# Dense attention rows by quarters of an image row, and a gate computed ahead of layer-norm statistics

## The chip, the cores and the metric

The kernel runs on one core of a Trainium2 chip. The time is that of the device, in microseconds: the median of several executions of the whole program. One further execution was taken with the hardware profiler; durations of single instructions come from it.

A core has a matrix engine (TensorE, "PE" in the profile, its weight loads "PEld"), a vector engine (DVE), a scalar engine (ACT), GpSimd (POOL), and SyncE (SP), which here only starts transfers. Transfers are started from SP's queue and from ACT's (SPq and ACTq) and carried out by 16 DMA engines. Each engine works through its own instructions in order and waits for the others by semaphores. A matmul multiplies a stationary operand, loaded first (LDWEIGHTS), with a moving one and writes to PSUM.

## The reference

The program is a chain of four blocks over `x[4, 64, 64, 128]`, all in float32. Two stages of it matter here. The first is the deformable attention of the first block: for each of 4 groups of 32 channels, a 3x3 neighbourhood with dilation `dil = 2 * i + 1` is shifted by learned offsets, keys and values are sampled there by bilinear interpolation, and a softmax over the 9 taps weighs the values.

```python
off = conv1x1(pconv(q_img, pconv_off_w[i]), w_off[i], b_off[i])
dil = 2 * i + 1
k_list.append(deform_sample(kv[0, :, i], off, mask, dil, dil * PAD))
v_list.append(deform_sample(kv[1, :, i], off, mask, dil, dil * PAD))
...
attn = jax.nn.softmax(jnp.einsum('bgnc,bgckn->bgnk', qf, ks_), axis=-1)
out = jnp.einsum('bgnk,bgckn->bgnc', attn, vs_)
...
return out @ w_proj + b_proj
```

The second is a triangle multiplication on the pair representation: `a` and `b` are gated projections of the normalized input `z`, `u` is their product summed over an index, and the output is the normalized `u` times `w_out`, times the sigmoid of `z @ w_gate`.

## The kernel before, in words

**Projection of the deformable part** (`deformable_project`). It computes queries, keys, values and offsets for the 4 images and stores them to DRAM: `qd`, `kd`, `vd`, `od`. `vd` holds the values with the image column first and a padded image row second, each row of 64 columns as two halves of 32; padding rows are zeroed at the start by ACT's queue (20 transfers), and the values are stored by ACT's queue, too (line 569, 8 stores per image).

**The local part** (`deformable_near`, about 660 to 1935 us in the profile). A test on the device takes this branch where all offsets are small. The unit of work is T, 128 queries: two image rows of 64. There are 32 per image, 128 in all, and four of them make a group c. The 128 partitions hold the queries as (column half h, row r, column in the half).

1. `products`, `product`, `copy_products`: queries times the keys around them. `product` (line 749) runs 64 small matmuls (32 x 32 stationary, 108 to 216 columns moving) per T, in two halves, into four PSUM tiles `S`; ACT copies them to `band` (line 759).
2. `hats`, `hat_products` (POOL): interpolation weights `H` from the offsets `of`.
3. `attention`, `spread` (DVE, one exponential on ACT): logits, softmax, and the 3 x W weights `A` of each query.
4. `write` (SP, line 821, 16 transfers per c): scatters `A` to the DRAM tiles `dd`, each query's weights at its own place on a row of zeros, so that they become a dense row over image columns. The rows cover 64 columns and some padding. `dd` is zeroed once at the start from a zeroed part of `dense` (line 665, 32 transfers).
5. `read_dense` (line 835): brings the dense rows back to SBUF for two T at once, as `dense` (tiles `D`): 8 transfers, 4 from SP's queue and 4 from ACT's, each of 64 partitions and 204 to 240 KB.
6. `transpose` (line 864): 24 transposes per T (three tap rows ty, two column halves, four groups), through PSUM tiles `pt`, copied by ACT to `dt` (line 866, six copies of 128x512).
7. `value_block` (line 845): loads a block of 4 image rows of values as `vb` (512 KB, one transfer, contiguous runs of 4 KB; 20 blocks per image, 9 buffers).
8. `weigh` (line 876): 24 matmuls of 128 rows (4 image rows of 32 columns: the columns of one half) x 32 channels x 128 queries per T, accumulated in `out` in PSUM. A float32 matmul shows as two records of the profile.
9. `values_done`, `projection`, `store`: once per c the output is copied, multiplied with `w_proj` (line 898), added to the input with POOL, and stored by SP (line 907). The result tile `pr` uses the transposes' PSUM buffers `pt`.

The order on each engine is written out by hand. Step T of the loop starts the loads and the DVE, POOL and ACT work that is due (`step`), then runs on PE, twice, once per half: transposes of T - LAG, product of T, projection if one is ready, weigh of T - LAG. `LAG = 13` is the distance between products and values. Before the first values the loop runs products alone, and after the last product, values alone (the drain).

**Triangle** (`stage_triangle`, about 2270 to 2670 us). Two passes `pr` over two images each: `zT` is the transposed normalized input, `u` is computed on PE, DVE takes its statistics (lines 1228 and 1229, 64 of each), PE transposes the normalized `u` (line 1241), and then for 16 groups PE computes `pg = zT * w_gate` and `po = uT * w_out` (lines 1253 and 1254), ACT the sigmoid `s` of `pg` (line 1259), DVE `s * po` (line 1260) and POOL adds it to `xs` (line 1261).

## Time and profile before

| what | value |
|---|---|
| median of 3 executions | 7821.81 us (7803.61 to 7821.86) |
| profiled execution | 7794.26 us, span 7792.5 us |
| mean granted TensorE clock | 0.907 of full |
| PE, DVE, ACT, POOL busy | 86%, 61%, 37%, 22% of the span |
| first transposes of the local part | 776 us |
| last product of the local part | 1835 us |
| end of the local part's values | about 1935 us |
| triangle's last stretch (second pass) | 2637 to 2668 us |

The page gives for the whole span the busy time of each engine, the granted clock and the DMA share in 40 slices of 195 us (slices 4 to 10 are the local part), the groups of instructions by line, and the transfers by queue. Since stages differ in what limits them, a stage is read through its own window: the busy time of each engine in 100 us, the waits by line inside it, and the sequence of work on PE. A row of the timeline begins with the start in us and the length in us. In a row by line, the last part is the time the engine stood idle just ahead of the group, with what released it; "issue" means that nothing in the profile shows what it waited for.

### The profile page before, as it was taken

To read this page: it belongs to the slowest core of one execution; us is meant where nothing else is said; L and a number is where in the kernel's file an instruction comes from. 1 tells how busy PE (TensorE), PEld (TensorE's weight loads), DVE (VectorE), ACT (ScalarE), POOL (GpSimd) and SP (SyncE) were. 2 spreads that over 40 slices of the span, in tenths; PEclk is the share of its full clock that TensorE was granted. 3 is DMA by queue.
4 is the path that set the end of the run, shared out by engine and by line. 5 is a ranking of instruction groups with operands and counts; after the bars stand their busy time and mean duration, and the time that the engine had idled before them with its cause. 6 is when DMAs were issued, how large, how long until landed. Compare 5 with 4: busy or idle time off the path is not lost. (4 is left out here: it accounts for less than half of the span.)

```text
span 7792.5 us, 166207 instructions
## 1 busy us (share of the span) xinstructions
PE 6724.8 (86%) x67663; PEld 3662.9 (47%) x67663; DVE 4726.2 (61%) x11050; ACT 2881.2 (37%) x6529; POOL 1720.3 (22%) x1638
## 2 busy tenths in 40 slices
PE   7985888897668878979999999798798897997989
PEld 3343666675445555335555555444325224243244
DVE  2113555553447743858866666575685885867877
ACT  3421444444324432731126565475204013031056
POOL 0004343331001110015542222144112012121135
PEclk9997999999678989989999999799798997998989
DMA  4346777876140013030100000001111111111101
GB/s 111 93 107 197 186 198 189 205 199 171 55 144 1 2 37 62 8 116 22 26 18 9 10 10 9 9 1 29 35 26 40 33 25 48 26 37 38 25 22 30
DMA packets 655282, 508.22 MB, mean 65 GB/s; under 512 B 302662, under 2 KB 594441, under 8 KB 650665
## 3 DMA queue, kind: packets, MB, share of 16 engines
q1 hardware_dynamic: 454158, 350.46, 17.4%
q10 hardware_dynamic: 200346, 146.97, 7.4%
q8 instruction: 540, 8.85, 0.5%
q14 instruction: 238, 1.94, 0.1%
HBM read 340.52 MB, written 156.58 MB: 64 GB/s over the span
## 5 line engine op out<-in xcount | busy, mean ns | idle before, releaser
L2457 DVE TENSOR_TENSOR t<-S,q 128x1536 f32<-128x1536 f32 (+3 forms) x608 | 1157.0, 1948 | 121.1 <-PE S L2445 115.8
L2445 PE MATMUL S<-R,L 32*128 32x512 f32 x4096 | 734.4, 651 | 91.0 <-DMA R<-wd 79.8
L2473 PE MATMUL acc<-t,sum 128*32 128x512 f32 x4096 | 639.7, 608 | 0.0
L866 ACT COPY dt<-pt 128x512 f32<-128x512 f32 x768 | 404.0, 594 | 440.9 <-PE pt L864 337.5
L768 DVE COPY_PREDICATED band<-bit,band 128x288 f32<-128x288 int32 (+11 forms) x384 | 246.1, 754 | 434.2 <-ACT band L759 434.2
L2159 PE MATMUL pe<-ew,yT 128*128 128x512 f32 x1024 | 480.6, 604 | 25.1 <-DVE xs L2165 22.2
L1758 PE MATMUL acc<-w,attT 128*64 128x264 f32 x4096 | 486.0, 391 | 12.2 <-DVE w L1754 12.2
L2445 PEld LDWEIGHTS S<-R,L 32*128 32x128 f32 x4096 | 200.8, 187 | 612.0 <-issue 281.5
L749 PE MATMUL S<-kpad,qm 32*32 32x108 f32 (+3 forms) x16384 | 380.3, 323 | 119.2 <-issue 51.9
L2479 ACT COPY agg<-acc 128x512 f32<-128x512 f32 x32 | 18.7, 585 | 1194.3 <-DMA L<-pd 682.2
L864 PE MATMUL pt<-ident,D 128*128 128x128 f32 x3072 | 441.7, 297 | 5.1 <-issue 2.9
L864 PEld LDWEIGHTS pt<-ident,D 128*128 128x128 f32 x3072 | 389.4, 199 | 60.8 <-issue 46.7
L1751 POOL TENSOR_TENSOR w<-xtl,ei 128x528 f32<-128x528 f32 x256 | 331.7, 1317 | 313.7 <-ACT ei L1750 202.9
L2165 DVE SCALAR_TENSOR_TENSOR xs<-pe,gate,xs 128x128 f32<-128x128 f32 x1024 | 332.6, 345 | 97.0 <-PE pe L2159 80.3
L1754 DVE TENSOR_TENSOR w<-xtl,pe 128x1056 f32<-128x1056 f32 x256 | 320.3, 1251 | 101.6 <-ACT ei L1750 89.5
L1758 PEld LDWEIGHTS acc<-w,attT 128*64 128x64 f32 x4096 | 284.1, 137 | 198.5 <-DVE w L1755 37.9
L2168 ACT ACTIVATE sc<-pe,gate 128x128 f32<-128x128 f32 x1024 | 290.4, 374 | 200.2 <-PE pe L2159 193.1
L749 PEld LDWEIGHTS S<-kpad,qm 32*32 32x32 f32 x16384 | 234.3, 106 | 198.6 <-issue 97.9
L512 PE MATMUL dw<-pad,diag 32*32 32x512 f32 x6912 | 307.4, 616 | 10.5 <-ACT dwo L520 5.8
L2488 POOL TENSOR_TENSOR o<-o,bf 128x512 f32<-128x512 f32 x32 | 40.6, 1269 | 1230.4 <-ACT o L2487 1230.4
L2473 PEld LDWEIGHTS acc<-t,sum 128*32 128x32 f32 x4096 | 92.9, 108 | 457.6 <-issue 435.2
L2159 PEld LDWEIGHTS pe<-ew,yT 128*128 128x128 f32 x1024 | 186.1, 194 | 231.5 <-issue 151.2
(520 smaller groups left out, 12848.3 us busy)
## 6 DMA issues: line engine op xcount, KB each, us to landing
vb<-vd SPq DMA_DIRECT2D x80, 512.0 KB
w<-in_e_weight_dram ACTq DMA_DIRECT2D x16, 1024.0 KB
w<-in_e_weight_dram SPq DMA_DIRECT2D x16, 1024.0 KB
wd<-s SPq DMA_DIRECT2D x32, 512.0 KB
D<-dd ACTq DMA_DIRECT2D x64, 240.0 KB
D<-dd SPq DMA_DIRECT2D x64, 240.0 KB
D<-dd ACTq DMA_DIRECT2D x64, 228.0 KB
D<-dd SPq DMA_DIRECT2D x64, 228.0 KB
```

The lines of the kernel that those rows point to most:

```text
L512: nc.tensor.matmul(acc[g][32 * c : 32 * c + 32], diag[r, j, tap, :], pads[j][r, y0 : y0 + 8, tx : tx + 64], start=(tap == 0), stop=(tap == 8),
L749: ins = nc.tensor.matmul(acc[g][32 * j : 32 * j + 32].rearrange("p (a s) c -> p a s c", a=3), qm[rows, j, m, :], keys, start=(m == 0), sto ...
L864: ins = nc.tensor.transpose(pt[:, g, :], D[g][:, T % 2, q0 : q0 + 382 : 3], k.ident)
L866: nc.scalar.copy(dt, pt)
L1751: nc.gpsimd.tensor_tensor(w2[:, 2:4], xt[:, 2:4, 0:2], window(ei, 0, [[0, 2], [0, 2], [1, 132]]), op=ALU.mult)
L1754: nc.vector.tensor_tensor(w1, xt[:, :, 1:3], window(pe, 0, [[0, 4], [0, 2], [1, 132]]), op=ALU.mult)
L1758: nc.tensor.matmul(acc[b // 2][64 * (b % 2) : 64 * (b % 2) + 64], attT[:, b // 2, hp, 64 * (b % 2) : 64 * (b % 2) + 64], src[:, b].rearran ...
L2159: nc.tensor.matmul(pe[h].rearrange("p e c -> p (e c)"), yT[:, 128 * t : 128 * t + 128], ew[:, 4 * h : 4 * h + 4, :].rearrange("p e c -> p ...
L2165: nc.vector.scalar_tensor_tensor(xt, pe[0][:, e, :], gate[:, t, e : e + 1], xt, op0=ALU.mult, op1=ALU.add)
L2445: nc.tensor.matmul(S[:, j, :], Ls[n % 2][r, ag, :], Rs[n % 2][r, ag].rearrange("p x y -> p (x y)"), start=True, stop=True)
L2457: nc.vector.tensor_tensor(t[:, j0:j1].rearrange("p u (x y) -> p u x y", x=8), S[:, j0:j1].rearrange("p u (x y) -> p u x y", x=8), qf[:, q0 ...
L2473: nc.tensor.matmul(acc[0][32 * h : 32 * h + 32, :], sum4, t[:, j, :], start=(u < 4), stop=(u >= 60))
```

## The change

Two independent parts.

*Local part.* The dense rows now cover 32 columns for 16 query columns (a quarter of an image row) in place of 64 for 32, so that the rows are 12 * (15 + W) numbers apart plus 12 in place of 12 * (64 + W). `read_dense` runs for each T: 4 transfers, one per group, on all 128 partitions, two from SP's queue and two from ACT's; the source is 8 blocks of 16 rows, with an offset of a whole row more from block to block. `dense` is four tiles, one per T. A T has 12 transposes and three copies. `weigh` runs 48 matmuls of 32 queries (two runs of 16), one per quarter, tap row and group, and leaves out those whose image rows lie outside. `vd` has the columns with 8 of padding on both sides, so that the 32 columns around each quarter are one stretch; `value_block` loads the four quarters by four transfers of 256 KB (runs of 2 KB), 17 blocks per image, 7 buffers. On PE a step is now: transposes, both halves of the product, projection, weigh. `LAG` is 14. The zeroing of `dd` and of `vd` and the stores to `vd` change with the layouts.

*Triangle.* The 64 `pg` matmuls of a pass and the sigmoids move from the last loop to the place ahead of `u`'s statistics; the sigmoid is written over `zT`, which gets a second buffer, and the tile `s` is gone.

```diff
--- before.py
+++ after.py
@@ -382,7 +382,7 @@
-        vd = [dr.tile([32, 84, 2, 128], F32, tag=f"vd{b}", name=f"vd{b}") for b in range(4)]
+        vd = [dr.tile([80, 84, 128], F32, tag=f"vd{b}", name=f"vd{b}") for b in range(4)]
         od = [dr.tile([128, 32, 81], F32, tag=f"od{b}", name=f"od{b}") for b in range(4)]
@@ -453,11 +453,13 @@
                 nc.vector.tensor_copy(wcen[0:32, :], pe[0:32])
         with tc.tile_pool(name="dp_z", bufs=1) as zp:
-            zero = zp.tile([32, 1024], F32, tag="zero", name="zero")
+            zero = zp.tile([64, 1536], F32, tag="zero", name="zero")
             nc.vector.memset(zero, 0.0)
             for b in range(4):
-                for r0, n in ((0, 4), (4, 4), (72, 4), (76, 4), (80, 4)):
-                    nc.scalar.dma_start(vd[b][:, r0 : r0 + n].rearrange("w r h c -> w (r h c)"), zero[:, 0 : 256 * n])
+                for c0 in (0, 72):
+                    nc.scalar.dma_start(bass.AP(vd[b].tensor, vd[b].offset + c0 * 10752, [[1536, 56], [1, 1536]]), zero[0:56])
+                for r0, n in ((0, 8), (72, 12)):
+                    nc.scalar.dma_start(vd[b][8:72, r0 : r0 + n].rearrange("w r c -> w (r c)"), zero[:, 0 : 128 * n])
@@ -565,10 +567,10 @@
                         vt[:, :, i, :].rearrange("p j (g c) -> p j g c", g=4), pt.rearrange("p g (j c) -> p j g c", j=4)
                     )
                 d = vd[b]
-                for yh in range(4):
+                for r in range(2):
                     nc.scalar.dma_start(
-                        bass.AP(d.tensor, d.offset + 256 * (32 * half + 8 + yh // 2) + 128 * (yh % 2), [[21504, 32], [512, 16], [1, 128]]),
-                        vt[32 * yh : 32 * yh + 32].rearrange("p j i c -> p (j i) c"),
+                        bass.AP(d.tensor, d.offset + 8 * 10752 + 128 * (32 * half + 8 + r), [[10752, 64], [256, 16], [1, 128]]),
+                        vt[64 * r : 64 * r + 64].rearrange("p j i c -> p (j i) c"),
                     )
             off = sm.tile([128, 32, 81], F32, tag="off", name="off")
     nc, tc = k.nc, k.tc
     DIL = (1, 3, 5, 7)
     W = [2 * d + 3 for d in DIL]
     WB = [5, 9, 15, 21]
     CW = [w + 7 for w in W]
-    PP = [12 * (64 + w) for w in W]
+    PP = [12 * (15 + w) for w in W]
@@ -653,16 +656,17 @@
-        dd = [[dr.tile([128, 4, PP[g]], F32, tag=f"dd{i}{g}", name=f"dd{i}{g}") for g in range(4)] for i in range(2)]
-
-        dense = [[wp.tile([128, 2, 768], F32, tag=f"D{i}{g}", name=f"D{i}{g}") for g in range(4)] for i in range(2)]
-        for t in dense[0] + dense[1]:
+        dd = [[dr.tile([128, 4 * PP[g] + 12], F32, tag=f"dd{i}{g}", name=f"dd{i}{g}") for g in range(4)] for i in range(2)]
+
+        dense = [wp.tile([128, 4, 384], F32, tag=f"D{i}", name=f"D{i}") for i in range(4)]
+        for t in dense:
             nc.gpsimd.memset(t, 0.0)
         for i in range(2):
             for g in range(4):
-                zero = dense[i][g].rearrange("p t n -> p (t n)")
-                for t in range(4):
-                    (nc.sync, nc.scalar)[g % 2].dma_start(dd[i][g][:, t, :], zero[:, 0 : PP[g]])
+                zero = dense[g].rearrange("p t n -> p (t n)")
+                eng = (nc.sync, nc.scalar)[g % 2]
+                eng.dma_start(dd[i][g][:, 0 : 4 * PP[g]], zero[:, 0 : 4 * PP[g]])
+                eng.dma_start(dd[i][g][:, 4 * PP[g] : 4 * PP[g] + 12], zero[:, 0:12])
@@ -817,66 +821,74 @@
             for g in (1, 2, 3, 0):
                 d, P = dd[c % 2][g], PP[g]
                 for j in range(4):
-                    h, r = divmod(j, 2)
+                    r = j % 2
                     nc.sync.dma_start(
                         bass.AP(
-                            d.tensor, d.offset + 32 * j * 4 * P + 3 * r + 12 * 32 * h, [[4 * P + 12, 32], [P, 4], [1, 12 * W[g]]]
+                            d.tensor, d.offset + 32 * j * (4 * P + 12) + 3 * r, [[4 * P + 12, 32], [P, 4], [1, 12 * W[g]]]
                         ),
                         A[g][32 * j : 32 * j + 32, :, 0 : W[g]].rearrange("p t c s a -> p t (c s a)"),
                     )
-        def read_dense(T2):
-
-            c, t2 = divmod(T2, 2)
+        def read_dense(T):
+            c, t = divmod(T, 4)
             for g, d in enumerate(DIL):
-                n = 12 * (33 + d)
-                for h in range(2):
-                    rows, c0 = slice(64 * h, 64 * h + 64), (768 - n) * h
-                    (nc.sync, nc.scalar)[h].dma_start(
-                        dense[T2 % 2][g][rows, :, c0 : c0 + n],
-                        dd[c % 2][g][rows, 2 * t2 : 2 * t2 + 2, 12 * (d + 1) + c0 : 12 * (d + 1) + c0 + n],
-                    )
+                m, P = dd[c % 2][g], PP[g]
+                (nc.sync, nc.scalar)[g % 2].dma_start(
+                    dense[t][:, g, 12 * (7 - d) : 12 * (7 - d) + P],
+                    bass.AP(m.tensor, m.offset + t * P, [[16 * (4 * P + 12), 8], [4 * P, 16], [1, P]]),
+                )
         def value_block(n):
-            b, kb = divmod(n, 20)
-            t = sm.tile([128, 4, 2, 128], F32, tag="vb", name="vb", bufs=9)
+            b, kb = divmod(n, 17)
+            kb += 1
+            t = sm.tile([128, 4, 4, 128], F32, tag="vb", name="vb", bufs=7)
             d = vd[b]
-            nc.sync.dma_start(
-                t.rearrange("p i h c -> p (i h c)"), bass.AP(d.tensor, d.offset + 4 * kb * 256, [[21504, 32], [256, 4], [1, 1024]])
-            )
+            for q in range(4):
+                nc.sync.dma_start(
+                    t[:, q].rearrange("p s c -> p (s c)"),
+                    bass.AP(d.tensor, d.offset + 16 * q * 10752 + 4 * kb * 128, [[10752, 32], [128, 4], [1, 512]]),
+                )
             vblocks[b, kb] = t
         def values(T):
             b, i = divmod(T, 32)
-            for n in range(len(vblocks), min(80, 20 * b + (2 * i + 14) // 4 + 1 + max(2, i - 27))):
+            for n in range(len(vblocks), min(68, 17 * b + min(17, (2 * i + 14) // 4) + max(2, i - 28))):
                 value_block(n)
             if T % 4 == 0:
                 outs[0] = ps.tile([128, 4, 128], F32, tag="out", name="out")
-        def transpose(T, half):
-            D = dense[T // 2 % 2]
+        def transpose(T):
+            D = dense[T % 4]
             lefts[T] = []
-            for q in range(3 * half, 3 * half + 3):
+            for ty in range(3):
                 pt = ps.tile([128, 4, 128], F32, tag="pt", name="pt", bufs=3)
-                q0 = 384 * (q % 2) + q // 2
                 for g in range(4):
-                    ins = nc.tensor.transpose(pt[:, g, :], D[g][:, T % 2, q0 : q0 + 382 : 3], k.ident)
+                    ins = nc.tensor.transpose(pt[:, g, :], D[:, g, ty : ty + 382 : 3], k.ident)
                 dt = sm.tile([128, 4, 128], F32, tag="dt", name="dt", bufs=4)
                 nc.scalar.copy(dt, pt)
                 lefts[T].append(dt)
             return ins
-        def weigh(T, half):
+        def weigh(T):
             b, i = divmod(T, 32)
-            for q in range(3 * half, 3 * half + 3):
-                ty, h = divmod(q, 2)
-                for g, d in enumerate(DIL):
+            taps = {}
+            for g, d in enumerate(DIL):
+                for ty in (1, 0, 2):
                     kb, si = divmod(2 * i + (ty - 1) * d - 1 + 8, 4)
-                    ins = nc.tensor.matmul(
-                        outs[0][32 * g : 32 * g + 32, T % 4, :], vblocks[b, kb][:, si, h, 32 * g : 32 * g + 32], lefts[T][q % 3][:, g, :],
-                        start=(q == 0), stop=(q == 5),
-                    )
+                    if 1 <= kb <= 17:
+                        taps.setdefault(g, []).append((ty, kb, si))
+            quarter = lambda ap, q: ap.rearrange("p (h r q x) -> p h q r x", h=2, r=2, q=2)[:, q // 2, q % 2]
+            for q in range(4):
+                for n in range(3):
+                    for g in range(4):
+                        if n < len(taps[g]):
+                            ty, kb, si = taps[g][n]
+                            ins = nc.tensor.matmul(
+                                quarter(outs[0][32 * g : 32 * g + 32, T % 4, :], q), vblocks[b, kb][:, q, si, 32 * g : 32 * g + 32],
+                                quarter(lefts[T][ty][:, g, :], q), start=(n == 0), stop=(n == len(taps[g]) - 1),
+                            )
+            del lefts[T]
             return ins
         def values_done(T):
@@ -912,7 +924,7 @@
             if 0 <= n < 128 and n % every == 0:
                 do(n // every)
-        LAG = 13
+        LAG = 14
@@ -928,19 +940,19 @@
                 step(T, 4, attention, 4)
                 step(T, 7, spread, 4)
                 step(T, 9, write, 4)
-                step(T, LAG - 2, read_dense, 2)
+                step(T, LAG - 2, read_dense)
                 step(T, LAG, values)
             V, P = 0 <= T - LAG, T < 128
             late = list(stores)
-            for half in range(2):
-                if V:
-                    block(transpose, T - LAG, half)
-                if P:
-                    block(product, T, half)
-                if project:
-                    block(projection, *project.pop())
-                if V:
-                    block(weigh, T - LAG, half)
+            if V:
+                block(transpose, T - LAG)
+            if P:
+                block(product, T, 0)
+                block(product, T, 1)
+            if project:
+                block(projection, *project.pop())
+            if V:
+                block(weigh, T - LAG)
             with behind():
                 if late:
                     store()
@@ -1168,7 +1180,7 @@
             nc.scalar.dma_start(vec[:, i : i + 1], v.unsqueeze(1))
         for pr in range(2):
-            zT = big.tile([128, 2, 4096], F32, tag="zT", name="zT")
+            zT = big.tile([128, 2, 4096], F32, tag="zT", name="zT", bufs=2)
             for i in range(2):
                 b = 2 * pr + i
                 mv, r = k.ln_stats(sm, b, k.eps6)
@@ -1222,6 +1234,16 @@
                         else:
                             nc.vector.tensor_copy(dst, pu[rows])
+
+            gate = lambda im, g: zT[:, im, 512 * g : 512 * g + 512].rearrange("p (t c) -> p t c", t=4)
+            for im in range(2):
+                for g in range(8):
+                    pg = ps.tile([128, 4, 128], F32, tag="psA", name="pg")
+                    for j in range(4):
+                        t = 4 * g + j
+                        nc.tensor.matmul(pg[:, j, :], zT[:, im, 128 * t : 128 * t + 128], wg, start=True, stop=True)
+                    nc.scalar.activation(gate(im, g), pg, AF.Sigmoid)
+
@@ -1246,17 +1268,14 @@
             for im in range(2):
                 b = 2 * pr + im
                 for g in range(8):
-                    pg = ps.tile([128, 4, 128], F32, tag="psA", name="pg")
                     po = ps.tile([128, 4, 128], F32, tag="psU", name="po")
                     for j in range(4):
                         t = 4 * g + j
-                        nc.tensor.matmul(pg[:, j, :], zT[:, im, 128 * t : 128 * t + 128], wg, start=True, stop=True)
                         nc.tensor.matmul(
                             po[:, j, :], uT[:, im, 2 * t : 2 * t + 2, :].rearrange("p i j -> p (i j)"), wo,
                             start=True, stop=True,
                         )
-                    s = sm.tile([128, 4, 128], F32, tag="s", name="s")
-                    nc.scalar.activation(s, pg, AF.Sigmoid)
+                    s = gate(im, g)
                     nc.vector.tensor_tensor(s, s, po, op=ALU.mult)
                     nc.gpsimd.tensor_tensor(k.xs[b][:, 4 * g : 4 * g + 4, :], k.xs[b][:, 4 * g : 4 * g + 4, :], s, op=ALU.add)
```

## The prediction

> **What bounds the kernel now.** I read the page's time slices first, then the windows by stage, the PE timeline inside one window, the groups by line, the waits, the queues, and last the triangle's timeline. Changes of 0.3% or less (23 us) count as no change: about what a measurement of this kernel can tell.
>
> The deformable part's loop runs from 776 us (first transposes) to 1835 us (last product): 1059 us for 115 steps T, 9.2 us each. Windows of it (columns: length, busy time of PE, PEld, DVE, ACT, POOL, granted clock, DMA share, GB/s):
> ```profile
> 1000.00:1100.00 100.00, 89.74 (x2305) 69.56 (x2300) 55.70 (x146) 49.70 (x122) 45.93 (x58) 1.00 0.82 208
> 1300.00:1400.00 100.00, 89.06 (x2224) 69.97 (x2224) 52.51 (x142) 48.22 (x119) 38.93 (x58) 0.93 0.79 204
> 1835.00:1935.00 100.00, 77.91 (x1040) 56.20 (x1040) 18.64 (x54) 46.73 (x92) 14.36 (x10) 0.96 0.60 146
> ```
> PE is busy for 86 to 90% with DMA close behind at 0.8; DVE and ACT have half their time free. One undisturbed half step on PE:
> ```profile
> 1319.02 1.63 PE L864 MATMUL pt<-ident,D 128*128 128x128 f32 x12
> 1320.58 1.33 PE L749 MATMUL S<-kpad,qm 32*32 32x108 f32 x64
> 1321.84 0.86 PE L876 MATMUL out<-dt,vb 128*32 128x128 f32 x24
> 1322.63 1.63 PE L864 MATMUL pt<-ident,D 128*128 128x128 f32 x12
> ```
> Start to start: transposes 1.56, product 1.26, weigh 0.79; a half is 3.61, a step 7.2, with a quarter of the projection (1.08 per four steps) 7.5. The other 1.7 us of 9.2 are a granted clock under 1 (about 0.5 per step, from the clock rows) and stalls of PE, among them a refill of its instructions (the rows ending in "issue" below) and what waits for late transfers:
> ```profile
> L866 ACT COPY dt<-pt 128x512 f32<-128x512 f32 x588 | 309.1, 594 | 342.2 <-PE pt L864 265.2 <-DMA vb<-vd 55.0 <-DMA D<-dd 20.2
> L749 PE MATMUL S<-kpad,qm 32*32 32x108 f32 (+3 forms) x12547 | 280.9, 311 | 39.6 <-issue 39.5
> L876 PE MATMUL out<-dt,vb 128*32 128x128 f32 x4704 | 183.9, 287 | 18.3 <-issue 18.1
> L898 PE MATMUL pr<-wpj,oT 128*128 128x128 f32 x192 | 35.5, 340 | 42.7 <-ACT dt L866 40.7 <-issue 2.0
> ```
> (900 to 1800 us; last columns: busy, mean ns, idle before and releaser.) ACT waits 75 us for `vb` and `D`, and the projection, which shares the transposes' PSUM buffers, pays 41 us of it.
>
> **The loop, part by part.** *PE.* Per step 12 transposes go instead of 24: one 1.56 stays. The product's 128 records stay, in one piece: 2.3 (2x1.26 less one change of kind of matmul, 0.2 to 0.27). Weigh has 96 matmul records of N=32 for 48 of N=128. No row shows N=32. Upper bound: what a record takes now, 0.79 less a change, 0.2, over 24 records = 25.7 ns, 2.5 us per step; lower: four records on four row groups start about 7 ns apart in the records, 0.7 us. The nearest row is the product, also small matmuls on column groups, 64 in 0.99 us = 15.7 ns: 1.5+0.2 = 1.7 us. With the projection's 0.27: 1.56+2.3+1.7+0.27 = 5.8 us (5.0 to 6.6), plus the clock's 0.4: 6.2.
>
> The Trainium skill, "TensorE: Matmul & The Clock Gate", section "Back-to-back issue gap", puts a floor of about 25 ns under each small matmul. By it weigh costs 2.4 us and a step 0.7 more; the records at 7 and 15.7 ns on separate groups disagree, so I do not follow it.
>
> *Instructions.* A step has 48+256+96 = 400 matmul and weight-load records now and 24+256+192 = 472 then. The profile's instruction queue and its kind in 900 to 1800 us:
> ```profile
> q1 hardware_dynamic: 144403, 129.92, 56.3%
> q10 hardware_dynamic: 28198, 44.54, 20.5%
> q8 instruction: 155, 2.54, 1.3%
> ```
> (packets, MB, share.) 155 fetches serve 900/9.2 = 98 steps, 1.6 each, one per about 250 records. Stops of PE recur at that count; two fetches are never closer than 3.3 us and 5.8 us apart on average. After: 1.6x472/400 = 1.87 per step. At 3.3 us that is 6.2, at 3.9 it is 7.3, at the loop's mean 5.8 it is 10.9; but the mean includes time PE was slow for other reasons, so it is no latency. I take 3.9.
>
> *DMA.* Reads of `D` fall from 909 to 639 KB per step; `vb` grows from 80 transfers of 512 KB to 272 of 256 KB (41 to 71 MB in the stage). Packets get smaller: `D` runs of 960 to 1536 B for 1632 to 1920 B, `vb` 2 KB for 4 KB. Summed by the mean time of packets of near sizes (1920 B 132 ns, 1296 B 70, 816 B 50, 4 KB 215), the load per step goes from 7.2 us of each engine to 6.2 (5.4 to 6.7). But the new source pattern of `D` has 8 as its outermost size where the old one had 64 rows. The trace has one place with such a pattern, pair attention's loads `L` and `R` from 8 rows (5700 to 5900 us):
> ```profile
> q10 hardware_dynamic: 9216, 1.58, 4.1%
> L<-pd ACTq DMA_DIRECT2D x64, 8.0 KB
> R<-wd ACTq DMA_DIRECT2D x32, 32.0 KB
> ```
> 9216 packets are 64x64 and 32x128 of data and 1024 = 64x8+32x16 of four bytes that close each engine's share: `L` ran on 8 engines, not 16. If `D` does so, those 8 carry its 3.4 to 4.6 us per step, 1.4 to 2.0 of `vb` and some 2 to 2.2 of the rest: 6.8 to 8.8, the other 8 about 3.8. Middle 7.8.
>
> The skill's "DMA: Bandwidth & Descriptors", section "Why a DMA increments its semaphore by 16 and not by 1", says the number of engines is the largest up to 16 that divides the outermost sizes of both sides. By it `D` is on 8, which would make the upper half of that bound sure; it speaks against the change.
>
> *Others.* ACT loses three of six 594 ns copies: -1.8 of 5.6 us per step. Its two `D` issues (0.59 each, 127 us for 196) stay per step on average, but every step instead of four every second. DVE is untouched: 55% of 9.2 is 5.1 per step. SP gets 192 more `vb` issues at 0.54 (104 us over 128 steps, 0.8 each) on 4.5: 5.3. It now waits in other places:
> ```profile
> SPq L821 <- DMA D<-dd: 117.0, 132, 3.1
> SPq L907 <- POOL xg L901: 97.4, 24, 7.7
> SPq L835 <- PE pt L864: 94.4, 82, 4.4
> ```
> The writes' wait for old reads of `dd` (117 us in 900) remains, as does the wait for PE. `vb` has 7 buffers where 5 are live: its issue waits for weigh two steps back, and behind it on SP queue the `D` reads and the stores. Price: none while `D` is read two steps ahead; up to one transfer's lateness per block (2 us per two steps, 1 per step) if that cover is gone.
>
> The bounds stand close together: PE 6.2, fetch 7.3, eight engines 7.8, SP 5.3. A loop with several near-equal resources now runs 9.2 where its largest single one, PE with its clock, is 8.0; taking a smaller slip on a bound of 7.8 I get 8.0 (7.2 to 9.8). 114 steps x 8.0 = 912 for 1059: **-147**.
>
> **Around the loop.** *Drain* (1835 to 1935): 13 steps in 100 us, 7.7 each. Without product, transposes 1.56, a copy's wait 0.6, weigh 1.7, projection 0.3: 4.2 by PE, 6.0 by the 8 engines (`D` and `vb`). 14 x 5.1 = 72: **-28** (-10 to -40).
>
> *Prologue.*
> ```profile
> 665.66 32.88 SPq L665 DMA_DIRECT2D dd<-D  x16
> 698.95 4.12 PE L749 MATMUL S<-kpad,qm 32*32 32x108 f32 x128 [20.13 <-ACT band L759]
> ```
> Zeroing `dd` holds both issue queues for 32 us (14.7 MB at 398 GB/s); ACT's first copy waits behind it and PE with it. It becomes 5.1 MB, 13 us: -18. One more step of lag, +6: **-12** (-18 to 0).
>
> *Start.* `vd` zeroing grows from 2.6 to 5.4 MB beside first loads that fill the engines at 243 GB/s; stores of `vd` halve in number, on ACT, 0.7 each. **+4** (-2 to +10).
>
> *Triangle.*
> ```profile
> 2598.11 3.96 PE L1253 MATMUL pg<-wg,zT 128*128 128x128 f32 x32
> 2617.49 2.27 PE L1241 MATMUL ptu<-ident,u 128*128 128x128 f32 x8 [15.42 <-DVE u L1238]
> 2637.20 6.51 PE L1254 MATMUL po<-wo,uT 128*128 128x128 f32 x40 [1.32 <-ACT uT L1242]
> L1261 POOL TENSOR_TENSOR xs<-xs,s 128x512 f32<-128x512 f32 x16 | 20.2, 1271 | 167.7 <-DVE s L1260 167.6
> ```
> While DVE takes u's statistics PE waits 15 us; the 16 `pg` groups (0.9 each, 14.4 us) fit there. PE starts the first few already, limited by two PSUM buffers. The end, 2637 to 2667, then has `po` alone: about 15 us of PE in the first pair, POOL's 20.3 in the second for 29. Gain 13+8 less a little of the 4 us done early: **-20** (-28 to -8). If the sigmoids delay ACT, the square root behind them is next.
>
> **Sum.** -147-28-12+4-20 = -203. The profiled execution has 7794.3 us (span 7792.5), 27.6 under the median of the runs shown: 7591 against it, 7619 as a median.
>
> **Rivals.**
> 1. *The eight engines saturate* (step 9.2, by the upper end 8.8 plus 0.4 clock): loop -10, total about -65, 7757. For it: `L`'s 8 shares. Against: half the `D` bytes per step are gone.
> 2. *PE and DVE set the step*, weigh near 7 ns, 7.2 us: loop -238, drain -36, total about -300, 7520. Against it: fetches at 7.3.
> 3. *Slower: instruction refill bounds PE.* 1.87 fetches per step at 5.45 us, as in crowded stretches, make 10.2: loop +104, others -38, 7888. It decides from 9.7 us a step (114x9.7 = 1106, +47, which eats the rest). For: refills share engines with `D`. Against: they are as long as the engines are crowded, and bytes fall.
> 4. *No net change*: step about 9.7.
>
> **Chances.** Forecast 0.45, rival 1 0.17, rival 2 0.17, rival 3 0.15, rival 4 0.06: faster 0.79, same 0.06, slower 0.15. The range runs from rival 2 with the triangle's and drain's best ends (7500) to a step of 9.7 to 9.8 (7850); the forecast's own, steps of 7.6 to 8.6, is 7570 to 7690.
>
> **What would show it.** Weigh's 96 records in 1.5 to 1.9 us; transposes of successive steps 7.6 to 8.6 us apart; per-engine packet counts split over 8 engines for `D`; PE stops at refills; zeroing of `dd` in 13 us; `pg` inside the statistics. Wrong if weigh takes 2.5 us, or ACT's copies wait for `D` or `vb` more than 0.75 us a step.

## The result

The change makes the kernel faster: 7718.5 us median of 4 executions (7702.8 to 7738.1) for 7818.3 us (7803.6 to 7821.9), a ratio of 0.9877 with a 95% interval of 0.985 to 0.9904, or 99.8 us. The forecast was 7619 us: the direction was right and the time lies inside the range, but the gain is half of the one forecast.

The two profiled executions differ by only 56 us (spans 7792.5 and 7736.3 us), because the one before was 24 us under its median and the one after is 20 us above its own. Most of that difference sits in stages which the change doesn't touch, the last row here. From the first matmul of a stage to the first of the next:

| stage | before | after | difference |
|---|---|---|---|
| projection of the deformable part | 660.5 | 674.1 | +13.6 |
| local part | 1287.3 | 1191.3 | -96.0 |
| expert choice (unchanged) | 309.4 | 305.1 | -4.3 |
| triangle | 395.4 | 378.3 | -17.1 |
| recurrent (unchanged) | 216.9 | 233.1 | +16.2 |
| all that follows (unchanged) | 4908.4 | 4939.9 | +31.5 |

The table's first five rows sum to -87.6 us; the last row is the scatter of the two executions (the same stages, with the code of before, take 4931.8 us in tri_only). Inside the local part the prologue (first product to first transposes) went from 100.9 to 81.4 us, the loop (to the last product) from 1060.9 to 996.2, the drain (to the last weigh) from 88.7 to 77.2. A step of the loop takes 996.2/114 = 8.74 us for 9.23.

Windows of the loop after, with the columns as before:

```profile
1000.00:1100.00 100.00, 72.76 (x2660) 58.58 (x2662) 46.87 (x147) 31.48 (x86) 45.93 (x58) 0.91 0.74 212
1300.00:1400.00 100.00, 70.76 (x2645) 55.92 (x2648) 50.96 (x159) 30.05 (x85) 41.64 (x55) 0.90 0.76 211
```

PE is busy for 71 to 73 us of 100 in place of 89, no other engine is over 51, DMA is at 0.75. Nothing is full, and yet a step takes 8.7 us. The timeline of PE shows what it does in the rest:

```profile
1216.79 2.83 PE L867 MATMUL pt<-ident,D 128*128 128x128 f32 x12
1219.55 2.70 PE L753 MATMUL S<-kpad,qm 32*32 32x108 f32 x128
1222.18 1.42 PE L887 MATMUL out<-dt,vb 128*32 128x32 f32 x91
1225.22 0.26 PE L887 MATMUL out<-dt,vb 128*32 128x32 f32 x5 [1.62 <-issue]
1225.41 1.63 PE L867 MATMUL pt<-ident,D 128*128 128x128 f32 x12
1226.97 2.10 PE L753 MATMUL S<-kpad,qm 32*32 32x108 f32 x110
1230.53 0.60 PE L753 MATMUL S<-kpad,qm 32*32 32x216 f32 x18 [1.46 <-issue]
1231.07 1.16 PE L910 MATMUL pr<-wpj,oT 128*128 128x128 f32 x8
1232.15 1.03 PE L887 MATMUL out<-dt,vb 128*32 128x32 f32 x96
```

PE stops in the middle of a row of equal matmuls, with nothing that the profile shows to wait for ("issue"), and it does so at every 255 or so records of matmuls and weight loads: here at about 1223 and 1229 us. An uninterrupted weigh (the last row) takes 1.0 us for 96 records. From the groups by line, 900 to 1700 us:

```profile
L753 PE MATMUL S<-kpad,qm 32*32 32x180 f32 (+3 forms) x11648 | 272.4, 338 | 76.9 <-issue 61.7 <-POOL qm L722 9.2 <-ACT band L763 4.6
L867 PE MATMUL pt<-ident,D 128*128 128x128 f32 x1083 | 183.1, 327 | 17.5 <-ACT o L912 10.8 <-issue 4.8 <-DMA D<-dd 1.8
L869 ACT COPY dt<-pt 128x512 f32<-128x512 f32 x273 | 148.1, 612 | 94.8 <-PE pt L867 94.1
L887 PE MATMUL out<-dt,vb 128*32 128x32 f32 x8477 | 123.1, 207 | 111.0 <-issue 110.9
L763 ACT COPY band<-S 128x108 f32<-128x108 f32 (+1 forms) x364 | 80.7, 308 | 404.6 <-DMA D<-dd 150.4 <-PE pt L867 83.9 <-PE S L753 83.2
L910 PE MATMUL pr<-wpj,oT 128*128 128x128 f32 x184 | 31.5, 321 | 4.6 <-issue 4.6
```

"issue" is now 182 us of 800 (61.7 + 4.8 + 110.9 + 4.6), where before it was 62 of 900. ACT's copies to `dt` no longer wait for `vb` or `D`, and the projection no longer for ACT. But ACT's copies of the products (L763) now stand 150 us behind `D`, 1.6 us a step, because ACT starts two of its reads in every step; the prediction had named more than 0.75 us as a sign of being wrong. What this wait is worth, sp shows below. The queues of the same window:

```profile
q1 hardware_dynamic: 154784, 129.47, 57.7%
q10 hardware_dynamic: 24874, 31.45, 13.6%
q8 instruction: 167, 2.74, 1.5%
```

167 refills in 800 us: one per 4.8 us and, at 91.5 steps, 1.83 per step. That the two multiply to the step says nothing by itself; that the refills set it is what the experiments had to show. From the records of that queue a refill is made of three parts: from PE's going on to the next packet's start at least 1.06 us (median 1.78), the packet 1.14 on average, and from its end to PE's going on 1.40 (median). Without any wait that is 3.6 us. PE needs about 2 us for 255 records of product and weigh, and 2.8 with transposes and projection among them (1.56 + 2.3 + 1.0 + 0.27 us a step, over 1.83). At 121 of the 167 PE stands still until the packet has landed, and between two such refills in a row 4.9 us pass on average.

The triangle's last pass after:

```profile
2507.16 14.08 PE L1244 MATMUL pg<-wg,zT 128*128 128x128 f32 x120
2526.55 2.27 PE L1263 MATMUL ptu<-ident,u 128*128 128x128 f32 x8 [5.31 <-DVE u L1260]
2546.34 3.99 PE L1274 MATMUL po<-wo,uT 128*128 128x128 f32 x32 [1.32 <-ACT uT L1264]
2550.81 11.78 PE L1274 MATMUL po<-wo,uT 128*128 128x128 f32 x96 [0.47 <-DVE zT L1279]
```

`pg` now fills PE's wait for DVE's statistics (5.3 us left of 15.4), and the last stretch of PE is 16 us long, from 2546.3 to 2562.6, where it was 27.

At the start, ACT's queue is held by the zeroing of `vd` for 25 us, 13.4 to 38.4, where it was 12:

```profile
13.36 0.79 ACTq L460 DMA_DIRECT2D vd<-zero  x2
14.19 3.37 ACTq L462 DMA_DIRECT2D vd<-zero  x2
...
35.21 3.12 ACTq L462 DMA_DIRECT2D vd<-zero  x2
```

### The profile page after: what moved, and what is told of

The parts are those of the page before. It is cut to its first block, busy times and chain, and to the rows that moved or that the text cites. A ratio compares the mean times of both kernels' runs of the same rounds, so it can differ in the third digit from the quotient of the medians.

```text
span 7736.3 us, 173919 instructions
## 1 busy us (share of the span) xinstructions
PE 6558.9 (85%) x71983; PEld 3546.3 (46%) x71983; DVE 4660.1 (60%) x11050; ACT 2675.9 (35%) x6141; POOL 1763.9 (23%) x1634
## 5 line engine op out<-in xcount | busy, mean ns | idle before, releaser
L753 PE MATMUL S<-kpad,qm 32*32 32x216 f32 (+3 forms) x16384 | 392.9, 344 | 141.1 <-issue 72.2
L753 PEld LDWEIGHTS S<-kpad,qm 32*32 32x32 f32 x16384 | 277.1, 111 | 226.4 <-issue 124.4
L887 PE MATMUL out<-dt,vb 128*32 128x32 f32 x12000 | 176.4, 207 | 154.8 <-issue 143.9
L763 ACT COPY band<-S 128x108 f32<-128x108 f32 (+3 forms) x512 | 113.5, 308 | 558.9 <-DMA D<-dd 188.5
L867 PE MATMUL pt<-ident,D 128*128 128x128 f32 x1536 | 257.6, 326 | 29.1 <-ACT o L912 11.0
```

The lines of the kernel that those rows point to most:

```text
L753: ins = nc.tensor.matmul(acc[g][32 * j : 32 * j + 32].rearrange("p (a s) c -> p a s c", a=3), qm[rows, j, m, :], keys, start=(m == 0), sto ...
L867: ins = nc.tensor.transpose(pt[:, g, :], D[:, g, ty : ty + 382 : 3], k.ident)
```

## The experiments

The step of the loop is measured in each run's profile as the time from the first transposes to the last product over the number of steps; the time between refills comes from the instruction queue's records in the middle of the loop, and refills per step are the step over that time. The ratio is to runs of before on the same chip as the run (medians 7818.3 us for the change, 7809.5 for near_only, tri_only, late_zero and d16, 7800.2 for wide, 7818.4 for sp and best1). near_only and late_zero have the same loop as the change; their steps differ from its by up to 0.06 us.

| run | median, us | ratio to before | step, us | refills a step | between refills, us |
|---|---|---|---|---|---|
| before | 7818.3 | 1 | 9.23 | 1.58 | 5.83 |
| the change | 7718.5 | 0.9877 (0.985 to 0.9904) | 8.74 | 1.83 | 4.78 |
| near_only | 7722.0 | 0.9887 (0.9857 to 0.9916) | 8.76 | 1.84 | 4.76 |
| tri_only | 7809.2 | 0.9994 (0.9978 to 1.0011) | 9.26 | | |
| late_zero | 7705.9 | 0.9858 (0.9827 to 0.9889) | 8.80 | 1.84 | 4.78 |
| d16 | 7704.5 | 0.986 (0.983 to 0.9889) | 8.73 | 1.84 | 4.74 |
| wide | 7682.2 | 0.9837 (0.9809 to 0.9866) | 8.45 | 1.44 | 5.86 |
| no_d | 7572.4 (one) | | 7.85 | 1.84 | 4.26 |
| no_vb | 7664.6 (one) | | 8.16 | 1.85 | 4.42 |
| no_d_vb | 7524.1 (one) | | 7.36 | 1.85 | 3.98 |
| sp | 7710.2 | 0.9872 (0.9842 to 0.9903) | 8.58 | 1.80 | 4.76 |
| wide_sp | 7702.9 (one) | | 8.44 | 1.45 | 5.84 |
| wide_no_d_vb | 7417.3 (one) | | 6.37 | 1.49 | 4.28 |
| best1 | 7686.9 | 0.9837 (0.9809 to 0.9864) | 8.76 | 1.84 | 4.75 |

**The two parts by themselves.** near_only is the change with the old `stage_triangle`; tri_only is the kernel before with the new one.

> The change without its triangle part. In the profiles the triangle part is worth 13 us (its end is 100.3 us earlier than before, its first matmul 86.7) and the local part with its projection 87. If the two parts add, this kernel is 85 to 90 us faster than before, some 13 us slower than the whole change. If the triangle part also shortens what follows, or costs there, the difference is over 25 or under 0.

> The kernel before with the triangle part alone. If it adds to the rest: 13 us faster than before (0.17%), and not the 20 us of the prediction.

near_only came out 87 us faster than the runs of before on its chip (7722.0 for 7809.5), as expected. tri_only is the same as before: 0.4 us, interval -17 to +9. Yet its profile shows the triangle 21 us shorter (374.5 for 395.4 from its first matmul to the next stage's). The recurrent stage behind it is 15.5 us longer (232.4 for 216.9), and it is 230 to 233 in the change, late_zero and d16 as well, but 218.4 in near_only. The reason is in DVE's work. The recurrent stage needs 64 statistics of the last pair of images (0.26 + 0.16 us each), which follow the triangle's additions; before, DVE had taken 58 of them by the triangle's last addition, in the pauses that PE left it there; with the shorter end it has taken 17. The other 41, 17 us of DVE, now hold up the next stage. ACT, between statistics and tiles, shows it, first before and then in tri_only:

```profile
2715.62 0.32 ACT L79 ACTIVATE ln_rstd<-ln_mv,eps 128x32 f32<-128x32 f32 x1
```

```profile
2688.06 0.32 ACT L79 ACTIVATE ln_rstd<-ln_mv,eps 128x32 f32<-128x32 f32 x1 [3.84 <-DVE ln_mv L77]
2711.51 0.32 ACT L79 ACTIVATE ln_rstd<-ln_mv,eps 128x32 f32<-128x32 f32 x1 [5.72 <-DVE ln_mv L77]
```

It now stands idle for 3.8 and 5.7 us until DVE's last statistics are there. The two stages together leave a gain of 5 us, well within the interval, which doesn't rule out the 13 us expected either.

**The zeroing at the start.**

```diff
-        with tc.tile_pool(name="dp_z", bufs=1) as zp:
-            zero = zp.tile([64, 1536], F32, tag="zero", name="zero")
...
+        def padding(b):
+            for c0 in (0, 72):
+                nc.sync.dma_start(bass.AP(vd[b].tensor, vd[b].offset + c0 * 10752, [[1536, 56], [1, 1536]]), zero[0:56])
...
                 store(depthwise(1, half), kd[b], half)
+            padding(b)
```

> The whole change, with the zeroing of vd's padding (16 transfers, 5.4 MB) moved from the start of ACT's queue to SP's queue inside the projection's loop, four transfers per image, behind the stores of the keys. In the profile of the change ACT's queue is held by these transfers from 13.4 to 38.4 us and the first matmul after the weights is at 41.1 us instead of 28.0. Theory (zeroing delays the first image's loads): the first of these matmuls comes at 18 to 28 us and the whole is 13 to 20 us faster than the change. Rival (the first loads are late for their own size): less than 4 us.

The first projection matmul starts at 25.7 us for 43.4, and the projection takes 645.3 us for 674.1. The loop's step came out at 8.80 in this run. The whole is 12.6 us under the change's median, just short of the 13 to 20 expected, and both medians scatter by that much; the 17.7 us at the start are plain in the profile.

**Eight engines or sixteen.**

```diff
-                    bass.AP(m.tensor, m.offset + t * P, [[16 * (4 * P + 12), 8], [4 * P, 16], [1, P]]),
+                    bass.AP(m.tensor, m.offset + t * P, [[4 * P, 16], [16 * (4 * P + 12), 8], [1, P]]),
...
+            mixed = lambda ap, q: ap.rearrange("p (x h r q) -> p h q r x", h=2, r=2, q=2)[:, q // 2, q % 2]
...
-                                quarter(lefts[T][ty][:, g, :], q), start=(n == 0), stop=(n == len(taps[g]) - 1),
+                                mixed(lefts[T][ty][:, g, :], q), start=(n == 0), stop=(n == len(taps[g]) - 1),
```

> The whole change, but the dense rows are read with the 16 columns outermost and the 8 blocks inside, so that the outermost size is 16 and not 8; partitions are in the order (column, block) and weigh picks its 32 columns of dt with a stride of 8 instead of two runs of 16. Theory A (instruction refills set the step: 1.84 refills of 4.8 us each, and the refill's DMA engine is one of those that D leaves free now): D comes to share that engine, the refill's wait ahead of its packet rises from 1.2 us to some 2 (before: 2.5), and the step grows from 8.7 to 9.3 or more, 70 us or more slower than the change. Theory B (the eight engines that carry D are the bound): the load per engine falls to 6.2 us a step and the step falls to 8 or less, 80 us or more faster.

Neither theory holds. ACT's queue shows that the spread did change: it carries nothing but `D` there, and the 256 transfers of the local part end with 4096 four-byte packets, 16 each, where in the change 256 end with 2048, 8 each. (The Trainium skill, "DMA: Bandwidth & Descriptors", section "Why a DMA increments its semaphore by 16 and not by 1", takes the number of engines as the largest up to 16 that divides the outermost sizes of both sides, 8 in the change and 16 here; the trace agrees.) But the step stays at 8.73 us, the time between refills at 4.74. Eight loaded engines are not the bound of the loop, and with `D` on all sixteen a refill's wait ahead of its packet is hardly longer (median 1.9 us for 1.8). The records don't say on which engine a refill runs, so whether it was one of the free ones stays open. Only the drain gained, 5 us (72.1 for 77.2).

**Fewer instructions, same columns.**

```diff
-            for q in range(4):
+            half = lambda ap, q: ap.rearrange("p (h x) -> p h x", h=2)[:, q // 2]
+            for q in (0, 2):
...
-                                quarter(outs[0][32 * g : 32 * g + 32, T % 4, :], q), vblocks[b, kb][:, q, si, 32 * g : 32 * g + 32],
-                                quarter(lefts[T][ty][:, g, :], q), start=(n == 0), stop=(n == len(taps[g]) - 1),
+                                half(outs[0][32 * g : 32 * g + 32, T % 4, :], q), vblocks[b, kb][:, q, si, 32 * g : 32 * g + 32],
+                                half(lefts[T][ty][:, g, :], q), start=(n == 0), stop=(n == len(taps[g]) - 1),
```

> The whole change, but weigh runs 24 matmuls of 64 queries (both quarters of a half against the values of the first) in place of 48 of 32, so that half of the queries are weighed with the wrong columns; columns streamed, transposes, copies and all transfers stay. A step has 376 matmul and weight-load records in place of 472. Theory A (refills of instructions set the step): 1.48 refills per step in place of 1.87 at the same 4.75 us between refills: step 7.0 to 7.4 for 8.74, loop shorter by 155 to 200 us. Theory B (transfers, or the columns streamed, set it): step 8.4 or more, loop shorter by less than 40 us.

Refills fell as expected, to 1.44 a step, but the step only to 8.45, between the two theories. Theory A alone is not enough: with a fifth of the refills gone, another limit shows 0.3 us behind the first.

**Fewer bytes, same instructions.** no_d returns from `read_dense` for T of 4 and more; no_vb allots and loads seven blocks and gives the later ones the same tiles; no_d_vb does both.

```diff
         def read_dense(T):
             c, t = divmod(T, 4)
+            if T >= 4:
+                return
...
+            if n >= 7:
+                vblocks[b, kb] = kept[n % 7]
+                return
             t = sm.tile([128, 4, 4, 128], F32, tag="vb", name="vb", bufs=7)
```

> The whole change, but the dense rows are read only for the first four T; later steps use those again. 639 KB a step less, and no transfer started by ACT in the loop. Theory A with refills slowed by crowded DMA engines: the time between refills falls from 4.75 to 4.2 to 4.5 us, step 7.8 to 8.3. Theory A with refills of fixed length: step 8.5 or more. Theory B (late D or ACT's held issues stop PE): step 7.5 or less with refills still as far apart as PE takes them.

> The whole change, but only the first seven blocks of values are loaded and used in turn: 71 MB and 244 issues on SP's queue less. Theory A with refills slowed by crowded DMA engines: 4.75 falls to 4.1 to 4.4 us, step 7.6 to 8.2. Theory A with refills of fixed length: step 8.5 or more. Theory B (late values, SP's queue): step 7.5 or less.

> Both left out: of the loop's transfers only the writes of dd and some 100 KB a step of others remain. Theory A with refills slowed by crowded DMA engines: the time between refills comes down to 3.5 to 3.9 us (3.3 is the least seen), step 6.5 to 7.2. Theory A with refills of fixed length: step 8.4 or more, for the PE instructions are the same. Theory B: the step falls to PE's own 5.8 to 6.2 with refills no longer in the way.

Refills per step stay at 1.84 to 1.85 in all three, so the step must fall as the time between refills does: 4.78, 4.42, 4.26, 3.98 us for 8.74, 8.16, 7.85, 7.36. What shows that refills are behind it is where PE stops and which part of the cycle gets shorter. PE still stops inside weigh and product, as in no_d_vb, where DMA is at a third of its time:

```profile
1199.90 2.02 PE L754 MATMUL S<-kpad,qm 32*32 32x108 f32 x108
1202.79 0.62 PE L754 MATMUL S<-kpad,qm 32*32 32x180 f32 x20 [0.87 <-issue]
1203.34 1.07 PE L893 MATMUL out<-dt,vb 128*32 128x32 f32 x96
...
1210.39 0.34 PE L754 MATMUL S<-kpad,qm 32*32 32x216 f32 x1 [1.06 <-issue]
```

The steps of the first two of these runs are where theory A with refills slowed by other transfers had them (no_vb's 4.42 us between refills is a little over its 4.1 to 4.4); the third missed it by little (7.36 for 6.5 to 7.2). The median from PE's going on to the next packet's start falls from 1.78 us to 1.47 (no_vb), 1.43 (no_d) and 1.21 (both), against a least of 1.05 to 1.07 in each run; the packet and what follows stay at 1.14 to 1.18 and 1.40. So other transfers lengthen a refill, and its fixed part of 3.6 us is most of it. They are not all of it: in wide, at the DMA share of the change (0.69 to 0.77), the median is 2.4 us, 5.0 in the 11 cases in which PE stopped for something else before the packet started and 2.2 in the other 45. Two more things change with the bytes. The runs also spare a queue its issues; for ACT's, sp below finds 0.16 us a step, for SP's no run tells. And the granted clock is higher (0.91 to 1.00 in no_d_vb, 0.83 to 0.91 in the change); no run separates what that is worth.

**The second limit.** In wide, PE stopped ahead of the product for ACT's copies of the product before (53 us of 700), while ACT stood at its two issues of `D` a step (waits of wide, 900 to 1600 us; total, times, longest):

```profile
ACT band L763 <- DMA dd<-A: 119.1, 21, 8.3
...
ACT band L763 <- DMA D<-dd: 92.2, 18, 10.0
...
PE S L753 <- ACT band L763: 53.2, 29, 6.3
```

sp and wide_sp start all reads of `D` from SP.

```diff
-                (nc.sync, nc.scalar)[g % 2].dma_start(
+                nc.sync.dma_start(
```

> The whole change, but all four reads of the dense rows are started by SP; in the change ACT starts two of them a step and stands at them (150 us in 700 for D itself, 33 for dd's writes) before it copies the product's result, which the next product needs. Theory C (refills come first, ACT's held issues are a second limit close behind): ACT's waits go, the step stays refill-bound at 8.4 to 8.74. Theory D (ACT's held issues are the first limit): step 8.0 or less, 80 us faster than the change. If SP, with 1.2 us a step more to issue, becomes the limit: slower than 8.8.

> The kernel with half as many, twice as wide matmuls in weigh (half of the queries get wrong columns), with all reads of the dense rows started by SP. With ACT starting them the step was 8.45 for 8.74, though refills fell from 1.83 to 1.45 a step; PE stopped ahead of the product for ACT's copies. Theory C: 1.45 refills at 4.8 us and no such stops, step 7.0 to 7.5. Theory E (what is left is crowded transfers, whoever starts them): step 8.2 or more.

sp came out as theory C has it: 8.58, refills at 4.76 us; its time is that of the change within the scatter. wide_sp did not: 8.44 for the 8.45 of wide. Theory C's second half falls. The wait only moved, to where the data is used (waits of wide_sp, 900 to 1500 us):

```profile
PE pt L867 <- DMA D<-dd: 79.5, 80, 4.7
PEld pt L867 <- DMA D<-dd: 68.2, 80, 3.8
```

PE stands at the transposes for `D`, 80 us in 600, 1.1 us a step. By these waits, what comes behind the refills, at about 8.4 us a step, is the arrival of the dense rows; no run takes `D` alone out of wide to confirm it. Whether SP's queue, the engines' load or the way from `write` to `read_dense` makes them late was not tried.

**Both limits out of the way.** wide_no_d_vb joins the edits of wide and no_d_vb.

> Reads of D and of the values left out as before (first four T, first seven blocks), and weigh with 24 wide matmuls in place of 48. Without these transfers the step was 7.36 with 1.85 refills of 3.98 us. Theory A or C (with transfers out of the way the number of PE instructions sets the step): 1.48 refills, 5.8 to 6.3 us. If PE's own work or another engine held that step: 7.0 or more.

```profile
1000.00:1100.00 100.00, 85.56 (x2957) 68.72 (x2950) 79.33 (x208) 42.50 (x118) 52.49 (x77) 0.98 0.42 99
```

6.37 us, a little over the expectation. With transfers out of the way, a fifth fewer instructions are worth 0.99 us a step (7.36 to 6.37), with them in the way 0.29. Now PE is at 86 and DVE at 79 us of 100: the work of engines is most of what is left (PE still stops at half of its refills).

**A version from these.** best1 joins late_zero and d16 and gives every second tile of the recurrent stage's normalization to ACT.

```diff
+            nb = sm.tile([128, 32], F32, tag="nb", name="nb", bufs=1)
+            nc.vector.scalar_tensor_tensor(nb, mv[:, :, 0], -1.0, rstd, op0=ALU.mult, op1=ALU.mult)
...
-                    k.ln_tile(y, b, 4 * g + j, mv, rstd)
+                    t = 4 * g + j
+                    if j % 2:
+                        nc.scalar.activation(y, k.xs[b][:, t, :], AF.Identity, bias=nb[:, t : t + 1], scale=rstd[:, t : t + 1])
+                    else:
+                        k.ln_tile(y, b, t, mv, rstd)
```

> The whole change with three edits: vd's zeroing late, dense rows read with 16 outermost, and in the stage behind the triangle every second normalized tile computed by ACT in place of DVE. In the change that stage is 233 us long for 217 before, since 41 of its 64 last statistics no longer run inside the triangle: DVE is the limit there. If that is so, the stage falls to 215 to 222 us and the whole is 30 to 40 us faster than the change (ratio to before 0.982 to 0.985). If DVE is not the limit there: 230 us or more, and 15 to 20 us faster by the other two edits.

The recurrent stage is 220.8 us for 233.1, as expected, and the whole 7686.9 us: 131 us under before on its chip, ratio 0.9837 (0.9809 to 0.9864), against 0.9877 for the change. By its ratio it is the fastest of the kernels that compute the whole, though its interval overlaps those of late_zero and d16 and, barely, that of the change.

## Why the prediction was right and wrong

- **The loop, the step that failed: "At 3.3 us that is 6.2, at 3.9 it is 7.3 ... I take 3.9."** The mechanism was seen, as one of several near-equal bounds, and the number of refills was right (1.87 forecast, 1.83 measured). The time of one was mis-sized: 4.78 us on average (4.9 between two at which PE stopped), which makes this term 8.74 us a step, the measured step, and not 7.3. 3.9 was a choice between the shortest gap (3.3) and the mean in the loop before (5.8), with no row for it; the fixed parts could have been read from the trace of before (at least 1.06 us, 1.18 and 1.40) and give 3.6 with no wait at all, which leaves 0.3 for the waits of a loop whose transfers were put at 6.2 us of each engine in a step of 8.0. The loop lost 64.7 us for the 147 forecast: 82 of the missing 103.
- **"eight engines 7.8", the bound that the forecast rested on,** was not one: `D` is on eight engines, and d16 shows that it costs the loop nothing.
- **Rival 3 (slower, refills bound PE)** had the mechanism and too high a price, 5.45 us each. Rival 1, priced at 7757, came closest in time for a wrong reason.
- **PE's own work** was forecast at 5.8 us a step. Weigh's 96 records, put at 1.7 us between 0.7 and 2.5, take 1.0: 10 ns each, nearer to the 7 ns of four row groups than to the product's 15.7. In the step no gain is left of it: PE stands 2.0 us a step at "issue" (182 us over 91.5 steps).
- **The drain**: -11.5 for -28. The old one was 88.7 us long from last product to last weigh; the 100 of the window held the last projection, too. The new one has 5.5 us a step for the 5.1 forecast.
- **The prologue**: -19.5 for -12 (zeroing `dd` took 13 us, 684.6 to 697.7, as forecast).
- **The start**: +13.6 for +4, over the range's +10. The 2.8 MB more were put beside other loads; in fact they stood ahead of the first images in ACT's queue, which late_zero shows.
- **The triangle**: about -17 to -21 in its own stage for -20, by the mechanism described. But the sum ended at the stage's last instruction: "If the sigmoids delay ACT, the square root behind them is next" asked about ACT and not about DVE, whose pauses in that stretch were in use by the next stage's statistics. tri_only measures the part at 0.4 us (-17 to +9).

## What to carry to other kernels

Where matmuls are short, count the instructions as well as the columns: here one refill of 255 records costs 3.6 to 4.8 us while PE works them off in 2 to 3 us. Splitting 24 matmuls into 48 cost 0.29 us a step as the loop stands (8.74 for the 8.45 of wide), and 0.99 with the transfers out of the way. An engine's idle time in a stretch may be another stage's work done early; before counting a stretch as shortened, look for whose instructions from later lines stand in its pauses. And constants at the front of a queue hold up whatever stands behind them: here 13 us more of zeroing put the first projection matmul 13 us later (43.4 us for 30.3).

## What the runs showed of the hardware

- A refill has a floor: in the loop of no run do two follow each other in less than 3.2 us, and its parts, without a wait, sum to 3.6 us (least 1.06, mean packet 1.14, median 1.40 after it). The Trainium skill, "Runtime: NRT & Kernel Launch", section "Instruction fetch mechanics", has the crossing from one block of 256 instructions to the next as mostly hidden. In this loop it is not: PE stops at 121 of 167, and stands 182 us of 800 at "issue"; the measurement decides.
- Between the runs, a lower granted clock goes with more stops of PE. The windows above have 0.91 and 0.90 after, at 71 to 73% busy, for 1.00 and 0.93 before at 89%; in no_d_vb, with shorter stops, it is 0.91 to 1.00. Summed over 900 to 1700 us, the time lost to a clock under 1 is 98 us after and 41 before. That the stops lower the clock is not shown: within the loop after, the two don't go together (75% busy at 0.83 from 1500 to 1600 us, 71% at 0.90 from 1300 to 1400).
